# Gathering shifted convolution images with 18 transfers instead of 24, and another order for the first steps, in a float32 network kernel

## The chip, the core and the metric

The kernel runs on one core of a Trainium2 chip. The metric is the device time of one execution in microseconds (us). The engines are named as in the profile: PE is TensorE's matmul stream and PEld its weight loads, DVE is VectorE, ACT is ScalarE, POOL is GpSimd, and SP is SyncE, which here does nothing but issue DMA transfers. A tile's partitions are its rows in on-chip memory; PSUM is the small memory that matmuls write into.

## The reference

Four layers act on an image batch `x` of shape (4, 32, 32, 16). Three of them are the same convolution layer with other weights, and each of these adds to `x` the following function of the normalized `x`:

```python
def conv_ref(inputs, M, W, G):                     # inputs: group-normalized x, NHWC
    first = einsum('ijyx,byxc->bijc', M, inputs)
    # every output place (i, j) has its own 3x3 kernel over 16 channels: 1024 * 16 filters
    shifted = conv(inputs, G)                      # (b, i, j, y, x, c)
    diff = relu(inputs[:, None, None] - shifted)
    second = einsum('ijyx,bijyxc->bijc', W, diff)
    return first - second
```

The layer between the second and the third convolution is an interval layer (scans and two small max-plus steps). It matters here only as other work that runs beside the second convolution.

## The kernel before, in words

The batch of 4 is split in two halves `g` of two images `b` each. There are six phases: convolution layer 0, 1 and 2, each for `g` = 0 and `g` = 1. A phase has 8 chunks `t` of 128 output places, and a chunk has 32 steps, one for each of 16 filters `f` and each of the two images. So a phase is 256 steps, and the whole kernel is 1536 steps. One step multiplies the image, unfolded by the nine taps of the 3x3 kernel, by 128 weight columns. The result `pc` (128 x 1024) is scaled by ACT (L711) and reduced against `W` by DVE in one instruction (L728, `junk`). Four PSUM pairs are there, so step `s` + 4 needs the reduction of step `s` to be done.

To keep float32 accuracy at the fast matmul format, weights and images are split into a high and a low part. Weights come in units of 4 filters, which serve 8 steps. `prep_parts` makes a unit's parts two units ahead: `upper` on DVE (L206), ACT copies, POOL subtractions and copies (L243 to L251), and then two transfers on SP that swap the partition halves (`parts<-parts`, L257), followed by the load of a later unit's raw weights (`raw<-in_g`, L111). The unit after that has the identity tap subtracted by POOL (L220, `prep`) before its own `upper`. The first two units are "plain": their weights are used unsplit, and the first 16 steps take longer matmuls.

The images of the next phase are made beside the steps of the current one. `before_conv` normalizes, writes the padded image to a DRAM tile `xs`, and gathers it back into the tile `raw` of 128 partitions and three slots. Slots 0 and 1 hold eight taps (four groups of 16 channels for each half `h` of the image's width), and slot 2 holds the ninth tap four times over. Then `split`, `place` and `difference` make the high, low and difference images (`ia`, `ib`, `iyz`, and `im9` for the ninth tap).

All of this is one generator, `behind`, that is resumed between steps. `yield n` says how many steps to go before it is resumed. The order written by this generator is the program order on every engine's queue and on SP's. SP has one queue, which runs ahead on its own and stops only where a transfer waits for its data. So the gather's transfers (L419) stand in SP's order between the `parts<-parts` pairs and `raw<-in_g` loads of the weight units. For layers 0 and 1 the gather is written over 12 steps and followed by a pause of 12; for layer 2 it is 12 and 6.

At the start (L936 to L948, `rest_of_start`) the first image comes already unfolded from the host and is normalized in place. `sides` sets the image's edges, `normal` normalizes a slot, `minus_center` subtracts the identity tap from the weights, and `prep_plain_rest` finishes the ninth tap's weights. A few of these stand on DVE and POOL ahead of the first matmuls, and the rest are resumed between the first steps.

Of the kernel before, what the change touches and what calls it, by code (L numbers as in the profile page):

```python
# [16 lines left out]
B, H, C = 4, 32, 16  # L17
NG = 2
GB = B // NG
# [9 lines left out]
RUN = (H - 1) * WP + HW  # L29
LAST = (H - 1) * HW  # L30
TAPS = ((0, 1, 2, 3), (6, 7, 4, 5))
TEMP = 2 * 2 * GB * NH
ROWS = P // H
FU = 4
# [11 lines left out]
def net_kernel(ctx: ExitStack, tc: tile.TileContext, x, xq, xi, convs, iv_w, iv_b, out):  # L46
# [26 lines left out]
    nc = tc.nc  # L73
# [33 lines left out]
    def load_raw(u):  # L107
        if u < n_chunks * NU:
            n = u // NU
            raws[u] = wpool.tile([P, 3, FU, P], F32, tag="raw", bufs=RAWS, name=f"raw_{u}")  # L110
            nc.sync.dma_start(raws[u], convs[phases[n // NT][1]][2][n % NT, u % NU])  # L111
# [16 lines left out]
    raw = const.tile([P, 3, GB, PITCH], F32, name="raw")  # L128
# [48 lines left out]
    def halve(dst, src, mask):  # L177
        nc.scalar.activation(dst, src, AF.Copy, scale=mask[:, 1:2])  # L178

    def halve_rest(dst, src, mask):  # L180
        nc.vector.scalar_tensor_tensor(  # L181
            dst, src, mask[:, 0:1], dst.bitcast(F32), op0=ALU.mult, op1=ALU.add
        )
# [15 lines left out]
    def image(v, x):  # L199
        return v.rearrange("... (y x) -> ... y x", x=x)[..., :HW]  # L200
# [17 lines left out]
    def minus_center(eng, u, s, at, to):  # L218
        f0 = u % NU * FU
        eng.tensor_tensor(  # L220
            raws[u][:, s, at:to], raws[u][:, s, at:to],
            pick[s][:, f0 + at : f0 + to].unsqueeze(2).to_broadcast([P, to - at, P]),
            ALU.subtract,
        )
# [46 lines left out]
    def prep_plain(u, at=0, to=FU, eng=nc.gpsimd):  # L271
        plain_unit(u)
        prep(u, at, to, eng)
        halve(units[u][3][:, at:to], raws[u][:, 2, at:to], low_p)

    def prep_plain_rest(u, at=0, to=FU):
        halve_rest(units[u][3][:, at:to], raws[u][:, 2, at:to], low_p)

    def halves(temp, b):
        v = temp[:, :TEMP].rearrange("p (k s b n) -> p k s b n", k=2, s=2, b=GB)  # L280
        return v[:, 0, :, b], v[:, 1, :, b]

    def split(eng, g, b, temp, name, pause=IDLE):

        ty, tz = halves(temp, b)
        high = upper(image(raw[:, :2, b], WP), 2, f"x{name}{b}")
        yield 1
        for s in range(2):
            eng.tensor_tensor(
                image(tz[:, s], HW), image(raw[:, s, b], WP), image(high[:, s], HW), ALU.subtract  # L290
            )
            yield pause
            nc.scalar.activation(ty[:, s], high[:, s], AF.Copy, scale=EPS)  # L293

    def difference(eng, g, b, s, temp):
        ty, tz = (v.bitcast(F32)[:, s] for v in halves(temp, b))
        eng.tensor_tensor(iyz[g][:, s, b], ty, tz, ALU.subtract)

    def place(g, b, temp):

        parts = halves(temp.bitcast(F32)[:, :TEMP], b)
        da, db = (v[g].bitcast(F32)[:, :, b] for v in (ia, ib))
        for lo, hi in QUARTERS:
            for to, src in zip((lo, hi), parts):
                nc.sync.dma_start(db[to], src[hi])
        for h, (lo, hi) in enumerate(QUARTERS):
            for k, to in enumerate((lo, hi)):
                at = (2 * k * GB + b) * NH + HW * (1 - h)
                pitch = GB * NH + HW * (2 * h - 1)
                src = temp.bitcast(F32)[lo, at : at + 2 * pitch].rearrange("p (s n) -> p s n", s=2)  # L310
                nc.sync.dma_start(da[to, :, :LAST], src[:, :, :LAST])
        yield 1
# [82 lines left out]
    def before_conv(g, layer):  # L395
        xn = work.tile([P, NT, GC], F32, tag="xn", bufs=2, name=f"xn_{g}_{layer}")
        xns[g] = xn
        yield from group_norm(g, f"c{g}{layer}", xn, 1 if layer == 2 else 4)

        nc.vector.transpose(
            xt[g][:, :, 1 : 1 + H], xn
        )
        inner = xs[g][:, :, WP : WP + H * WP].rearrange("p h (t r n) -> p h r t n", r=ROWS, n=WP)
        for r in range(ROWS):
            for h in range(2):
                nc.sync.dma_start(
                    inner[:, h, r], xt[g][GC * r : GC * (r + 1), :, HW * h : HW * h + WP]
                )  # L410
        yield 2
        xsv = xs[g].rearrange("(b c) h n -> c h b n", b=GB)
        for slot, row, tap in [
            (slot, row, tap) for slot in range(2) for row, tap in enumerate(TAPS[slot])
        ] + [(2, row, 8) for row in range(4)]:
            for h in range(2):
                off = tap // 3 * WP + tap % 3
                r0 = 64 * h + C * row
                nc.sync.dma_start(  # L419
                    raw[r0 : r0 + C, slot ^ h if slot < 2 else 2, :, :RUN], xsv[:, h, :, off : off + RUN]  # L420
                )
            yield 1
        yield 6 if layer == 2 else 12
        temp = big.tile([P, 8192], F32R, tag="big", name=f"temp_{g}{layer}")
        for b in range(GB):
            yield from split(nc.gpsimd, g, b, temp, f"{g}{layer}")
            yield IDLE
            halve(image(im9[g][:, b], HW), image(raw[:, 2, b], WP), low_x)
            yield from place(g, b, temp)
            for s in range(2):  # L430
                difference(nc.gpsimd, g, b, s, temp)
            yield 1
            halve_rest(image(im9[g][:, b], HW), image(raw[:, 2, b], WP), low_x)
            yield 4
# [453 lines left out]
    off = const.tile([P, 1], F32, name="off")  # L888
# [21 lines left out]
    def sides(eng, b, slot, only=("left", "right", "top", "bottom")):  # L910

        v = raw[:, slot, b].rearrange("p (y x) -> p y x", x=WP)
        if slot == 2:
            at = v[64:, :, HW - 1]
            eng.tensor_scalar(at, at, mean0[64:, b : b + 1], None, op0=ALU.add)
        for side, at in (
            ("left", v[:, :, 0]), ("right", v[:, :, HW - 1]),
            ("top", v[:, 0, :HW]), ("bottom", v[:, H - 1, :HW]),
        ):
            if side in only and f"{side}{slot}" in keep:  # L920
                k = keep[f"{side}{slot}"]
                eng.tensor_scalar(  # L922
                    at, at, kept[:, k : k + 1], fill[:, b, k : k + 1], op0=ALU.mult, op1=ALU.add
                )

    def normal(eng, b, slot):
        v = raw[:, slot, b, :RUN]
        if eng is nc.scalar:
            eng.activation(v, v, AF.Identity, bias=minus_mean0[:, b : b + 1])
            eng.activation(v, v, AF.Copy, scale=rstd0[:, b : b + 1])  # L930
        else:
            eng.tensor_scalar(  # L932
                v, v, mean0[:, b : b + 1], rstd0[:, b : b + 1], op0=ALU.subtract, op1=ALU.mult
            )

    sides(nc.vector, 0, 0)  # L936
    sides(nc.gpsimd, 0, 2)
    minus_center(nc.gpsimd, 0, 1, 0, F0)
    sides(nc.gpsimd, 0, 1, ("left", "right"))
    nc.vector.reciprocal(rstd0, rstd0)  # L940
    normal(nc.scalar, 0, 2)
    normal(nc.vector, 0, 0)
# [7 lines left out]
    def rest_of_start():  # L950

        nc.sync.dma_start(X[0], x[0])
        load_raw(2)
        load_raw(3)
        prep_plain_rest(0, F0, FU)
        yield 1
        sides(nc.gpsimd, 1, 2)
        sides(nc.gpsimd, 1, 1, ("left", "right"))
        sides(nc.vector, 1, 0)
        sides(nc.vector, 1, 1, ("top", "bottom"))  # L960
        for eng, slot in ((nc.scalar, 2), (nc.vector, 0), (nc.vector, 1)):
            normal(eng, 1, slot)
        halve(image(im9[0][:, 1], HW), image(raw[:, 2, 1], WP), low_x)
        halve_rest(image(im9[0][:, 1], HW), image(raw[:, 2, 1], WP), low_x)
        prep_plain(1)
        prep(2)
        yield 1
        prep_plain_rest(1)
        yield 1
        temp = first.bitcast(F32R)[:, used:]  # L970
        for b in range(GB):
            yield from split(nc.vector, 0, b, temp, "00", 1)
            yield from place(0, b, temp)
            for s in range(2):
                difference(nc.vector, 0, b, s, temp)
            yield 1
        nc.gpsimd.memset(zero, 0.0)
        nc.vector.memset(part, 0.0)
        zeros(0)
        xns[0] = work.tile([P, NT, GC], F32, tag="xn", bufs=2, name="xn_00")  # L980
        yield from group_norm(0, "c00", xns[0], 4, CALM)
# [83 lines left out]
```

## Time and profile before

| | us |
|---|---|
| median of 3 runs (2466.83 to 2468.67) | 2467.36 |
| the profiled execution's own time | 2469.47 |
| its span, first to last instruction | 2467.4 |
| PE busy | 2457.5 (100%) |
| PE weight loads busy | 2056.1 (83%) |
| DVE busy | 2075.6 (84%) |
| ACT busy | 1873.6 (76%) |
| POOL busy | 1594.7 (65%) |
| DMA queue q1 (SP), share of 16 engines | 53.4% |
| granted PE clock | 1.000 |

Busy times are sums over an engine's instructions. PE's matmuls are pipelined and their ends are modelled, so a PE that is 100% busy can still lose time to waits; the steps' start times tell more. The DMA share is the time that packets took on 16 DMA engines. A "packet" of the profile is one run of bytes that one DMA engine moves.

### The profile page before, as it was taken

What the parts mean: (1) busy time and instruction counts of PE and PEld (TensorE: products, weight loads), DVE (VectorE), ACT (ScalarE), POOL (GpSimd) and SP (SyncE); (2) the same over time, 40 slices, a digit from 0 to 9 for tenths busy, and PEclk for the clock granted to TensorE, in tenths of its full rate; (3) what the DMA queues carried; (4) which work ended last, traced back from release to release, by engine and by line L of the source; (5) the groups of instructions that cost most, each with busy time, mean ns of one, the idle gap of its engine ahead of it and who ended that gap; (6) DMA issues with size and microseconds to landing.
All of it is one profiled execution on the core that took longest, in us unless ns stands there. A gap on an engine that the chain in (4) does not pass through costs nothing.

```text
span 2467.4 us, 58148 instructions
## 1 busy us (share of the span) xinstructions
PE 2457.5 (100%) x21928; PEld 2056.1 (83%) x21928; DVE 2075.6 (84%) x3631; ACT 1873.6 (76%) x2164; POOL 1594.7 (65%) x1864
## 2 busy tenths in 40 slices
PE   9999999999999999999999999999999999999999
PEld 5888888888888888888888888888889888888887
DVE  9888878888888888878898888888888888788887
ACT  4777777787777778767777777777777787677776
POOL 5767665676666667555576876776777675555552
PEclk9999999999999999999999999999999999999999
DMA  7456654485444467644554454664444476554452
GB/s 202 138 156 162 185 179 137 127 200 141 133 143 135 137 168 186 199 113 137 138 139 131 126 142 136 168 179 137 128 136 136 128 206 179 147 148 137 138 137 55
DMA packets 96906, 366.92 MB, mean 149 GB/s; under 512 B 25712, under 2 KB 30704, under 8 KB 96624
## 3 DMA queue, kind: packets, MB, share of 16 engines
q1 hardware_dynamic: 96064, 362.79, 53.4%
q8 instruction: 172, 2.82, 0.5%
q14 instruction: 110, 0.90, 0.1%
q10 hardware_dynamic: 432, 0.39, 0.1%
q0 software_dynamic: 128, 0.02, 0.0%
HBM read 199.78 MB, written 1.02 MB: 81 GB/s over the span
## 4 chain that ended last, share of the span: by engine, by line
PE 96%; DVE 1%; DMA 1%; ACT 1%; issue 1%; POOL 0%; ACTq 0%; DVEq 0%; POOLq 0%
PE pc L675 95%; PE pf L451 1%; DVE junk L728 1%; DMA raw<-in_g 0%; ACT pc L711 0%; DMA first<-in_g 0%; ACT temp L293 0%; PE ps_l L585 0%; DMA ib<-first 0%; PE ps_r L600 0%; DVE raw L922 0%; DVE im L181 0%; DVE W L181 0%; DVE raw L932 0%; ACT im L178 0%
## 5 line engine op out<-in xcount | busy, mean ns | idle before, releaser
L728 DVE SCALAR_TENSOR_TENSOR junk<-pc,WT 128x1024 f32<-128x1024 f32 x1536 | 1879.3, 1224 | 354.4 <-PE pc L675 295.2
L711 ACT ACTIVATE pc<-pc 128x1024 f32<-128x1024 f32 x1520 | 1532.2, 1008 | 560.5 <-PE pc L675 525.2
L675 PE MATMUL pc<-iyz,parts 64*128 64x512 f32 x6080 | 943.3, 387 | 2.1 <-ACT pc L711 1.6
L675 PE MATMUL pc<-ib,parts 64*128 64x512 f32 x6080 | 945.2, 387 | 0.2
L675 PE MATMUL pc<-ia,parts 64*128 64x496 f32 x6080 | 920.8, 379 | 0.0
L675 PEld LDWEIGHTS pc<-ia,parts 64*128 64x128 f32 x6080 | 578.8, 184 | 111.7
L675 PEld LDWEIGHTS pc<-ib,parts 64*128 64x128 f32 x6080 | 576.9, 184 | 108.4 <-issue 5.0
L675 PEld LDWEIGHTS pc<-iyz,parts 64*128 64x128 f32 x6080 | 577.3, 184 | 97.9 <-ACT pc L711 7.3
L675 PE MATMUL pc<-im,W 64*128 64x496 f32 x3072 | 598.6, 383 | 0.0
L243 POOL TENSOR_TENSOR parts<-raw,upper_w 128x512 fp32r<-128x512 f32 x190 | 249.5, 1313 | 522.7 <-DVE upper_w L206 440.9
L675 PEld LDWEIGHTS pc<-im,W 64*128 64x128 f32 x3072 | 292.7, 184 | 59.9 <-issue 3.3
L249 POOL CAST parts<-parts 32x512 fp32r<-32x512 f32 x380 | 231.7, 610 | 36.0 <-ACT parts L246 17.4
L247 POOL TENSOR_TENSOR parts<-parts 128x512 fp32r<-128x512 f32 x190 | 247.5, 1303 | 1.6 <-ACT parts L242 1.5
L244 POOL TENSOR_TENSOR W<-W,raw 128x512 fp32r<-128x512 f32 x190 | 247.8, 1304 | 0.3 <-ACT W L178 0.3
L251 POOL CAST parts<-upper_w 32x512 fp32r<-32x512 f32 x380 | 233.1, 613 | 22.8
L220 POOL TENSOR_TENSOR raw<-raw,ident 128x512 f32<-128x512 f32 x190 | 197.9, 1042 | 59.3 <-DMA raw<-in_g 35.4
L178 ACT ACTIVATE W<-raw,low_w 128x512 fp32r<-128x512 f32 x190 | 136.2, 717 | 3.7 <-DMA raw<-in_g 3.7
L728 DVE DVE_READ_ACCUMULATOR junk<-pc,WT 128x1 f32 x1536 | 127.6, 83 | 0.0
L242 ACT ACTIVATE parts<-upper_w 128x512 fp32r<-128x512 f32 x190 | 118.7, 624 | 3.8 <-DVE upper_w L206 3.7
L246 ACT CAST parts<-upper_w 128x512 fp32r<-128x512 f32 x190 | 116.1, 611 | 0.0
L743 POOL TENSOR_SCALAR acc<-acc 128x32 f32<-128x32 f32 x40 | 15.7, 392 | 133.9 <-DVE junk L728 132.1
L206 DVE TENSOR_SCALAR upper_w<-raw 128x512 int32<-128x512 int32 x190 | 82.1, 432 | 10.2 <-POOL raw L220 9.9
(158 smaller groups left out, 481.2 us busy)
## 6 DMA issues: line engine op xcount, KB each, us to landing
raw<-in_g SPq DMA_DIRECT2D x190, 768.0 KB, 7.2
parts<-parts SPq DMA_DIRECT2D x380, 384.0 KB, 5.0
WT<-in_w SPq DMA_DIRECT2D x48, 512.0 KB, 4.8
MT<-in_mt SPq DMA_DIRECT2D x24, 512.0 KB, 7.5
raw<-xs SPq DMA_DIRECT2D x120, 71.8 KB, 3.5
ib<-temp SPq DMA_DIRECT2D x40, 128.0 KB, 7.4
ia<-temp SPq DMA_DIRECT2D x40, 124.0 KB, 6.0
ib<-first SPq DMA_DIRECT2D x8, 128.0 KB, 4.0
```

Source lines behind the costliest of these rows:

```text
L178: nc.scalar.activation(dst, src, AF.Copy, scale=mask[:, 1:2])
L220: eng.tensor_tensor(raws[u][:, s, at:to], raws[u][:, s, at:to], pick[s][:, f0 + at : f0 + to].unsqueeze(2).to_broadcast([P, to - at, P]), ...
L242: nc.scalar.activation(WD, high, AF.Copy, scale=-EPS)
L243: nc.gpsimd.tensor_tensor(WL, w8, high, ALU.subtract)
L244: nc.gpsimd.tensor_tensor(W9, W9.bitcast(F32), src[:, 2], ALU.add)
L246: nc.scalar.copy(WU, high)
L247: nc.gpsimd.tensor_tensor(WD, WD.bitcast(F32), WL.bitcast(F32), ALU.add)
L249: nc.gpsimd.tensor_copy(WU[hi], WL[lo].bitcast(F32))
L251: nc.gpsimd.tensor_copy(WL[lo], high[hi])
L675: nc.tensor.matmul(ps[:, h, at : at + n], lhsT=w[r], rhs=v[r] if n == NH else v[r][:, :n], start=first and k == 0, stop=k == len(pairs) - ...
L711: nc.scalar.activation(ps, ps, AF.Copy, scale=1.0 + EPS)
L728: nc.vector.scalar_tensor_tensor(junk, ps.rearrange("p h n -> p (h n)"), 0.0, chunks[n], op0=ALU.min, op1=ALU.mult, accum_out=accs[phase][ ...
```

## The change

The gather in `before_conv` is rewritten. Before, each transfer moved one tap: 16 channels of both images into 16 partitions. Now adjacent groups of partitions whose taps lie at a constant distance are moved by one transfer for one image: three taps (48 partitions), one tap for both images as before (16 partitions), twice two taps (32 partitions), and the ninth tap's four copies (64 partitions). To do this, a leading dimension of 3, 2, 2 or 4 is put in front of the source's access pattern, with a distance of one element between taps, or of zero for the copies. That makes 18 transfers for each gather in place of 24 in the code before. For layers 0 and 1 they are written two for every second step, over 18 steps and with a pause of 6; for layer 2 two for each step, over 9 steps and with a pause of 9. The sum of the pauses is the same as before.

At the start, POOL sets the left and right edges of slot 1 before it subtracts the identity tap, not after. `prep_plain_rest(1)` comes one step later, and the differences of the first phase's two images come together after both images have been placed.

```diff
+RUNS = ((0, 0, 3, 0, 1), (0, 3, 1, 3, 1), (1, 0, 2, 6, 1), (1, 2, 2, 4, 1), (2, 0, 4, 8, 0))
...
-        for slot, row, tap in [
-            (slot, row, tap) for slot in range(2) for row, tap in enumerate(TAPS[slot])
-        ] + [(2, row, 8) for row in range(4)]:
+        for b, (slot, row, n, tap, by) in [
+            (b, run) for b in range(GB) for run in RUNS if run[2] > 1 or b == 0
+        ]:
             for h in range(2):
+                at = raw[64 * h + C * row :, slot ^ h if slot < 2 else 2, :, :RUN]
                 off = tap // 3 * WP + tap % 3
-                r0 = 64 * h + C * row
-                nc.sync.dma_start(
-                    raw[r0 : r0 + C, slot ^ h if slot < 2 else 2, :, :RUN], xsv[:, h, :, off : off + RUN]
-                )
-            yield 1
-        yield 6 if layer == 2 else 12
+                src = xsv[:, h, :, off : off + RUN]
+                if n > 1:
+                    src = src[:, b]
+                    src = bass.AP(src.tensor, src.offset, [[by, n]] + [list(d) for d in src.ap])
+                    dst = at[: n * C, b]
+                else:
+                    dst = at[:C]
+                nc.sync.dma_start(dst, src)
+            yield 1 if layer == 2 else 2
+        yield 9 if layer == 2 else 6
...
     sides(nc.gpsimd, 0, 2)
+    sides(nc.gpsimd, 0, 1, ("left", "right"))
     minus_center(nc.gpsimd, 0, 1, 0, F0)
-    sides(nc.gpsimd, 0, 1, ("left", "right"))
...
         prep(2)
-        yield 1
+        yield 2
         prep_plain_rest(1)
-        yield 1
...
             yield from place(0, b, temp)
+        for b in range(GB):
             for s in range(2):
                 difference(nc.vector, 0, b, s, temp)
             yield 1
```

## The prediction

> **What bounds the kernel now.** I read the page first: PE is busy for the whole span, and the chain that ended last is PE's for 96% of it.
>
> ```profile
> PE 2457.5 (100%) x21928; PEld 2056.1 (83%) x21928; DVE 2075.6 (84%) x3631; ACT 1873.6 (76%) x2164; POOL 1594.7 (65%) x1864
> PE 96%; DVE 1%; DMA 1%; ACT 1%; issue 1%; POOL 0%; ACTq 0%; DVEq 0%; POOLq 0%
> raw<-xs SPq DMA_DIRECT2D x120, 71.8 KB, 3.5
> ```
>
> The change removes no matmul, so it can only remove or add waits of PE. PE's timeline gives their size. An undisturbed step takes 1.57 us (a weight unit of eight: 12.54). From the starts of the 1536 steps I added what lies above that, leaving out the plain steps' longer matmuls, the `pf` matmuls and the interval layer: 3.4 us of waits in the first 52 us and some 5 us elsewhere, of which 1.4 at 920.7 and 0.2 to 0.4 each at a dozen places. So a gain is capped near 8 us (0.3%). A loss has no such cap.
>
> The last line is the gather: 120 transfers in five gathers, so 24 each (not 36). Its order on SP is seen in the DMA queue's timeline, here ahead of phase 4 (columns: start, us of issuing, line, transfer, count):
>
> ```profile
> 1562.49 1.11 SPq L257 DMA_DIRECT2D parts<-parts  x2
> 1563.64 1.91 SPq L111 DMA_DIRECT2D raw<-in_g  x1
> 1565.66 9.34 SPq L419 DMA_DIRECT2D raw<-xs  x14
> 1575.17 1.10 SPq L257 DMA_DIRECT2D parts<-parts  x2
> 1576.38 1.15 SPq L111 DMA_DIRECT2D raw<-in_g  x1
> 1577.57 9.35 SPq L419 DMA_DIRECT2D raw<-xs  x10
> 1587.08 1.11 SPq L257 DMA_DIRECT2D parts<-parts  x2
> ```
>
> The weight units' transfers stand behind gather transfers. PE's timeline shows how little room they have: the unit whose halves are swapped at 1575.17 starts here, 7.8 us later.
>
> ```profile
> 1582.96 0.62 PE L675 MATMUL pc<-ib,parts 64*128 64x512 f32 x4
> ```
>
> In a quiet stretch this distance is 14 to 15 us. Ahead of phase 3 (SP timeline, then the chain of waits) the same order already costs PE time:
>
> ```profile
> 896.28 11.86 SPq L419 DMA_DIRECT2D raw<-xs  x16
> 909.51 1.25 SPq L111 DMA_DIRECT2D raw<-in_g  x1
> ...
> 909.51 11.36 DMA raw<-in_g
> 921.01 1.05 POOL raw L220
> ```
>
> Sixteen gather transfers hold SP until 908.14; the load behind them lands at 920.87, POOL and DVE (`upper`, due at 919.27) wait, and PE loses the 1.4 us.
>
> Last, how transfers are spread, from the DMA view of 620 to 700 us (nothing is gathered there) and of 1565.6 to 1587:
>
> ```profile
> DMA packets 2138, 10.67 MB, mean 133 GB/s; under 512 B 327, under 2 KB 327, under 8 KB 2128
> parts<-parts SPq DMA_DIRECT2D x12, 384.0 KB, 4.4
> raw<-in_g SPq DMA_DIRECT2D x6, 768.0 KB, 7.0
> WT<-in_w SPq DMA_DIRECT2D x2, 512.0 KB, 4.5
> ...
> DMA packets 1585, 4.36 MB, mean 204 GB/s; under 512 B 437, under 2 KB 437, under 8 KB 1582
> q1 hardware_dynamic: 1582, 4.33, 75.3%
> ```
>
> 20 transfers leave 327 small packets, 16 each; the second window's 27 leave 437, again 16. So every transfer ends on 16 engines, and the outermost dimension of each, on both sides, is a multiple of 16 (partitions or channels).
>
> **The gather.** The bytes stay: 768 rows of 2296 B per gather. But the new sources begin with a dimension of 3, 2, 2 or 4. The trace has no such transfer, so I bound it: its rows are shared by all 16 engines (48 rows on each per gather, as now), or go through one engine (up to 768). Between these far ends I take equal slabs of the outermost dimension, because multiples of 16 in that place are what goes with 16 engines in every row: 16 rows on each of the first 3, 2, 2 or 4 engines. With (0,3,1) unchanged at 2 rows, the first two engines then carry 4 transfers x 4 runs x 16 + 4 = 260 rows per gather in place of 48. I take an engine's queue as served in order (the load of 909.51, behind sixteen gather transfers, took 11.36 us to land, against the page's median of 7.2), so the swaps and loads behind the gather wait for their share on these two.
>
> [...]
>
> A row's time on one engine: in 1565.6 to 1587 a packet takes 0.753 x 16 x 21.4 / 1585 = 0.163 us for 2.75 KB on average, or 0.136 for 2296 B; the window's best slices (394 GB/s, 24.6 per engine) give 0.093. Few engines draw at once, so I take 0.10, near the low end.
>
> Layer 2 (two gathers): the pauses put the first 7 of 9 entries, 14 transfers, where 14 stood, but with 6 x 2 x 16 + 4 = 196 rows on the first engine: 19.6 us (18.2 to 26.7). Its service starts at about 1567.5, behind the `raw<-in_g` of 1563.64, and ends at 1587.1; the swap's own rows (8 of 6 KB, about 2.4 us) and about 1.2 us to the signal make it 1590.7, where PE needs it at 1583.2. PE waits 7.5 us (6 to 15). The load behind it is as late, in the shadow of the same wait. The second batch (64 rows) fits in the next unit. Two gathers: **+15** (12 to 30). `split` reads the first image at 1590, 8 us after its rows.
>
> Layers 0 and 1 (three gathers): spread over 18 steps, 4, 8 and 6 transfers stand between the units' groups: 36, 128 and 96 rows, so 3.6, 12.8 and 9.6 us against a unit of 12.54 that also holds 4.4 us of the units' own rows. In phase 0, counting from 206.2, the swaps land near 231.0 and 245.0; PE starts those units at 230.82 and 243.35 (the second matmul pair needs them 0.2 later): 1.4 late. The other two gathers have about 1 us more room: some 1.4 together. **+2.8** (0 to 22). The 1.4 us at 920 go, because 8 transfers stand there instead of 16: **-1.4**. The images' own deadline (step 24) holds: last rows at about 241, second image split at 256.
>
> SP issues 30 transfers fewer at about 0.5 us; that is covered, as SP waits for data afterwards anyway.
>
> **The first steps.** Timeline: POOL waits until 7.62 for a load, subtracts until 8.53, then sets edges until 9.31; DVE's last edges and normalization follow, and PE's second matmul group idles 1.25 us until 10.55.
>
> ```profile
> 8.53 0.78 POOL L922 TENSOR_SCALAR raw<-raw,kept,fill 128x32 f32<-128x32 f32 x2
> 10.55 1.13 PE L675 MATMUL pc<-raw,first 64*128 64x512 f32 x4 [1.25 <-issue]
> 13.21 0.42 POOL L915 TENSOR_SCALAR raw<-raw,mean 64x32 f32<-64x32 f32 x1 [3.90 <-DMA raw<-in_xi]
> ```
>
> With the edges first (7.07 to 7.85) DVE normalizes by 9.2 and PE goes on at 9.3; the ninth tap's matmuls move from 11.56 to 10.45: 1.1 us. It is given back: the second image lands at 13.2 whatever is done before, DVE's chain from there (edges, normalization, ninth tap until 18.27, then the reduction of step 1 until 19.42) hardly moves, and step 5 waits for that reduction's PSUM pair, at 19.5 as against 19.66. Then the ninth weights (1.53 us on DVE) leave the place before step 2's reduction, but `upper` behind them waits for POOL's subtraction until 20.32: DVE idles 0.9. Step 6 starts 0.45 earlier; step 7, now behind the ninth weights, about 0.75 later. The differences (2.13 and 1.35 us on DVE) move four steps back and none; DVE has little slack until 51 us, so this only shifts who is late. Together **+0.5**, between -1.2 (all of the first gain stays) and +1.2.
>
> **Sum.** +15 + 2.8 - 1.4 + 0.5 = +16.9 us. The profiled execution took 2469.47, 2.1 more than its span and than the median; the waits add to each alike, so on the median 2467.4 + 16.9 = 2484.3.
>
> [...]
>
> **The rivals.** (1) The new transfers keep 16 engines. For: the same bytes and row size. Then 18 issues only relieve SP: -1.4 - 0.4 (small DVE waits in the two layer-2 gathers) + 0.5: 2466.1, no measurable change (about 0.2%, 4.9 us, is what a measurement of this kernel can tell from none). (2) Not slower but faster: as (1), and the gather's late data were also behind the dozen small waits. It needs most of the 8 us; the places at 260, 544 and 947 show ACT queued behind `split`'s copies, which stay in their steps: 2461. It decides if no row of a gather delays a unit. (3) One engine carries a whole new transfer: 516 rows instead of 196 in layer 2's batch, 32 us more twice, and about 38 in each of three: near 2660. Against it: only the outermost size sets it apart from all rows shown. (4) Fewer transfers than said: it is 24 to 18, not 36 to 18; this is already in the sum.
>
> **The numbers.** Forecast 0.77, (1) 0.17, (2) 0.04, (3) 0.02. The forecast's own range runs from 2477 (0.093 us per row, first gain kept: +12 + 0 - 1.4 - 1.2) to 2519 (0.136: +30 + 22 - 1.4 + 1.2). To hold 8 in 10 it reaches down to case (1): 2466 to 2520. Slower by over 0.2%: 0.77; within it, case (1) and the weakest end of the forecast against little else: 0.19; faster 0.04.
>
> **What would show it.** Right: `raw<-xs` x90 with a median landing far above 3.5 us; far fewer small packets than 16 for each of them; `parts<-parts` landings above 15 us in the gathers; PE idle before `ib` matmuls near 1583 and 1990 by 6 to 9 us each, and 1 to 2 us near 231 to 245; no wait at 921; first `im` matmul near 10.45 and step 7 later than 24.45. Wrong: 16 small packets for each gather transfer and landings below 5 us; then the time stays.

## The result, and the profile after

The changed kernel takes 2533.95 us (median of 5 runs, 2531.91 to 2536.75) against 2467.36 before: 1.027 times as long, 95% interval 1.0258 to 1.0282. The forecast was 2484.3, with a range up to 2520. The direction and the mechanism held, but the loss is 66.6 us and not 16.9.

The page of the changed kernel, from its busy times, DMA packets, chain and groups (in this kernel the lines stand up to six lower than before, so PE's L675 is L681):

```profile
PE 2480.4 (98%) x21928; PEld 2066.3 (82%) x21928; DVE 2083.8 (82%) x3631; ACT 1874.4 (74%) x2164; POOL 1596.8 (63%) x1864
DMA packets 95365, 366.91 MB, mean 145 GB/s; under 512 B 24172, under 2 KB 29164, under 8 KB 95084
PE 86%; DMA 8%; SPq 2%; DVE 1%; issue 1%; POOL 1%; ACT 0%; DVEq 0%; POOLq 0%; ACTq 0%
L681 PE MATMUL pc<-ib,parts 64*128 64x512 f32 x6080 | 964.8, 389 | 42.5 <-DMA parts<-parts 36.7
```

PE is no longer busy throughout, the chain that ended last holds 10% of DMA and SP (1% of DMA before), and PE stands idle ahead of the first matmuls that need swapped weights (`parts<-parts`). PE's waits over the whole span (total, times, longest) say the same; before, no wait of PE for `parts<-parts` was listed:

```profile
PE pc L681 <- DMA parts<-parts: 36.7, 12, 10.2
PE pc L681 <- DVE junk L734: 6.3, 10, 1.1
```

The gather ahead of phase 4, on SP's timeline; it answers to the lines from 1562.49 of before:

```profile
1599.66 2.39 SPq L258 DMA_DIRECT2D parts<-parts  x2
1602.09 0.59 SPq L112 DMA_DIRECT2D raw<-in_g  x1
1602.79 12.26 SPq L427 DMA_DIRECT2D raw<-xs  x14
1615.43 1.92 SPq L258 DMA_DIRECT2D parts<-parts  x2
1619.62 0.35 SPq L112 DMA_DIRECT2D raw<-in_g  x1
```

Then PE's timeline, the chain of waits there, and the DMA view of 1600 to 1640 (one character or number for each us):

```profile
1629.95 0.79 PE L681 MATMUL pc<-ib,parts 64*128 64x512 f32 x1 [9.37 <-DMA parts<-parts]
1631.53 0.79 PE L681 MATMUL pc<-ib,parts 64*128 64x512 f32 x1 [0.79 <-DMA parts<-parts]
```

```profile
1608.05 8.77 DMA raw<-xs
...
1616.84 14.65 DMA parts<-parts
```

```profile
DMA  5989988611123231599995961122299999962111
GB/s 110 198 203 197 227 362 296 175 73 78 67 80 96 83 104 78 162 213 271 200 134 216 319 190 52 51 67 87 81 210 226 221 201 332 239 184 95 59 53 56
```

The swap issued at 1615.43 lets PE go on only 14.5 us later. For long stretches ahead of it the DMA engines are 10 to 30% busy, the work of two to five of the sixteen, and move 50 to 100 GB/s. Where the number falls to about 50 it fits two engines at the 24.6 GB/s that each has in the best slices of before (394 GB/s over 16).

The page no longer gives a landing time for the gather's transfers, but the trace's semaphore updates do (the trace keeps the time of each update that a DMA makes). From issue to last update a gather transfer takes 12.6 us in the median, 3.5 before. Before, each has 16 updates. Of the 90 now, 10 have 16; each of the others has one about 1 to 2 us after its issue and then only 2 (40 transfers), 3 (20) or 4 (20) more. The swap issued at 1615.43 has all 16: thirteen within 4.1 us, one after 5.9, and the last two after 14.3 and 14.5. Read as one update for each engine that a transfer ran on, this says that two of the sixteen DMA engines hold up the whole swap.

What happens after such a wait is seen in PE's granted clock (the number after POOL's count), here around the same place:

```profile
1620.00:1630.00 10.00, 0.63 (x7) 0.21 (x3) 1.35 (x4) 0.73 (x1) 0.00 (x0) 0.71 0.52 141
1630.00:1633.00 3.00, 2.21 (x9) 1.45 (x11) 0.00 (x0) 0.00 (x0) 0.00 (x0) 0.50 0.97 216
1633.00:1636.00 3.00, 3.00 (x24) 2.46 (x22) 1.23 (x2) 1.61 (x2) 0.84 (x1) 0.77 0.93 252
1636.00:1640.00 4.00, 4.00 (x39) 3.15 (x35) 3.64 (x7) 3.61 (x6) 2.78 (x4) 1.00 0.17 66
```

PE restarts at clock 0.50 and has 1.00 again from 1634.36 on. At the other gathers a whole step of 2.84 to 2.95 us follows the wait where 1.57 is usual.

From the starts of all 1536 steps, the two profiles differ as follows (sum 64.2 of the spans' 64.6 us; PE's waits are those listed for the gather's window):

| stretch | later by, us | of it PE waits for swaps | for DVE |
|---|---|---|---|
| first 20 steps | 5.4 | - | - |
| gather ahead of phase 1 | 10.6 | 5.3 | 1.4 |
| phase 2 | 11.15 | 5.0 | 1.3 |
| phase 3 | 10.1 | 5.4 | 1.2 |
| phase 4 (layer 2) | 12.55 | 10.2 | - |
| phase 5 (layer 2) | 14.45 | 10.8 | - |

### The profile page after: what moved, and what is told of

The parts are those of the page before. It is cut to its first block, busy times and chain, and to the rows that moved or that the text cites. A ratio compares the mean times of both kernels' runs of the same rounds, so it can differ in the third digit from the quotient of the medians.

```text
span 2532.0 us, 58118 instructions
## 1 busy us (share of the span) xinstructions
PE 2480.4 (98%) x21928; PEld 2066.3 (82%) x21928; DVE 2083.8 (82%) x3631; ACT 1874.4 (74%) x2164; POOL 1596.8 (63%) x1864
## 4 chain that ended last, share of the span: by engine, by line
PE 86%; DMA 8%; SPq 2%; DVE 1%; issue 1%; POOL 1%; ACT 0%; DVEq 0%; POOLq 0%; ACTq 0%
PE pc L681 85%; DMA raw<-xs 4%; DMA raw<-in_g 2%; DMA parts<-parts 2%; DVE junk L734 1%; PE pf L457 1%; SPq L427 1%; SPq L409 1%; DMA first<-in_g 0%; DMA xs<-xt 0%; POOL raw L221 0%; ACT pc L717 0%; SPq L258 0%; POOL parts L250 0%; POOL parts L248 0%
## 5 line engine op out<-in xcount | busy, mean ns | idle before, releaser
L681 PE MATMUL pc<-ib,parts 64*128 64x512 f32 x6080 | 964.8, 389 | 42.5 <-DMA parts<-parts 36.7
L681 PE MATMUL pc<-iyz,parts 64*128 64x512 f32 x6080 | 957.2, 388 | 0.9 <-ACT pc L717 0.4
L681 PE MATMUL pc<-ia,parts 64*128 64x496 f32 x6080 | 937.0, 381 | 0.0
L681 PEld LDWEIGHTS pc<-ib,parts 64*128 64x128 f32 x6080 | 587.8, 185 | 160.4 <-DMA parts<-parts 42.0
L681 PEld LDWEIGHTS pc<-ia,parts 64*128 64x128 f32 x6080 | 589.3, 185 | 112.5
L681 PEld LDWEIGHTS pc<-iyz,parts 64*128 64x128 f32 x6080 | 586.0, 185 | 98.8 <-ACT pc L717 5.6
L681 PE MATMUL pc<-im,W 64*128 64x496 f32 x3072 | 609.9, 385 | 0.0
L681 PEld LDWEIGHTS pc<-im,W 64*128 64x128 f32 x3072 | 302.3, 185 | 60.3 <-issue 3.5
```

The lines of the kernel that those rows point to most:

```text
L681: nc.tensor.matmul(ps[:, h, at : at + n], lhsT=w[r], rhs=v[r] if n == NH else v[r][:, :n], start=first and k == 0, stop=k == len(pairs) - ...
```

## The experiments

The theory: a merged transfer runs on as many engines as its source's outermost size (2, 3 or 4, the number of its later updates), so its rows take long on those, and the weight units' swaps and loads, which stand behind it in SP's queue, come late. Rivals: it is the order or the pauses, the number of transfers, or the first steps. "Gather" below means the change's gather with its pauses in the kernel before. Ratios are against the kernel before.

**The two halves of the change.** First the gather alone, then the three first-step edits alone, each as in the diff of the change.

> The kernel before with the gather and its pauses alone changed. Theory (few DMA engines carry the new transfers): nearly all of the loss is here. In the profile of the changed kernel the five gathers cost 10.3, 10.9, 9.7, 12.1 and 13.9 us more than before, together some 57 to 59, so 2524 to 2527. Rival (the first steps hold a good part of the loss, because they shift the whole schedule): clearly less, below 2515.

2531.86 us, ratio 1.0255 (1.024 to 1.027), somewhat above the expected range. From its waits of PE:

```profile
PE pc L681 <- DMA parts<-parts: 38.7, 15, 9.8
```

> The kernel before with the three edits of the first steps alone. Theory: the 5.4 us by which step 20 starts later in the changed kernel's profile stay, so 2471 to 2474. Rival (PE's slower first matmuls in that profile were a chance of that one execution): within 1.5 us of before, 2466 to 2469.

2473.59 us, ratio 1.0021 (1.0012 to 1.003); 5.0 us are lost by step 20. The halves add up to the whole. The 1.4 us wait at 921 of before is missing here too, where nothing of the gather is changed, and in each of the four first-step runs below; so its going isn't the gather's doing.

**Same transfers, other order of the source's dimensions.** The runs' 48, 32 or 64 partitions stay; only the 16 channels become the source's outermost dimension. (Taps and channels then land in each other's partitions, so this kernel times the transfers and doesn't compute the reference.)

```diff
-src = bass.AP(src.tensor, src.offset, [[by, n]] + [list(d) for d in src.ap])
+src = bass.AP(src.tensor, src.offset, [list(src.ap[0]), [by, n], list(src.ap[1])])
```

> As gather_only, with the first two dimensions of each new source exchanged: 16 channels first, then 2, 3 or 4 taps. Number of transfers, bytes, rows, partitions, order and pauses stay. Taps and channels land in each other's partitions, so the convolutions of phases 1 to 5 multiply the wrong pairs. [...] Rival (large transfers for one image, the new order, or the pauses are what costs): still above 2510.

2468.68 us, ratio 1.000 (0.999 to 1.0009): the gather's loss is gone; 2464 to 2468 was expected by the theory. No wait of PE for swaps is left, there are 1060 more small packets than in the changed kernel, and the gather's transfers have a landing time in the page again (KB, us):

```profile
DMA packets 96425, 366.91 MB, mean 149 GB/s; under 512 B 25232, under 2 KB 30224, under 8 KB 96144
raw<-xs SPq DMA_DIRECT2D x50, 71.8 KB, 5.6
raw<-xs SPq DMA_DIRECT2D x20, 143.5 KB, 5.1
```

That is the count which the theory gives: 40 pairs, 20 triples and 20 runs of four that leave 2, 3 and 4 small packets each, and 16 each with the channels outermost, differ by 40 x 14 + 20 x 13 + 20 x 12 = 1060. All 90 transfers have 16 semaphore updates again. So in these runs the source's outermost size decides (2, 3 and 4 against 16 updates); the order, the pauses and these 18 larger transfers cost nothing by themselves.

**Transfers of one tap and one image.** 46 for each gather, each with 16 channels outermost.

```diff
-dst = at[: n * C, b]
+for k in range(n):
+    one = bass.AP(src.tensor, src.offset + k * by, [list(d) for d in src.ap])
+    nc.sync.dma_start(at[k * C : k * C + C, b], one)
...
-nc.sync.dma_start(dst, src)
```

> As gather_only, each run of n taps issued as n transfers of 16 partitions for one image, in the same places of the order: 46 transfers per gather instead of 18. Theory: every transfer has 16 channels outermost and runs on 16 engines; SP spends about 14 us more on issuing per gather than with 18, so 2466 to 2475. Rival (order, pauses or one image at a time): above 2510.

Missed: 2506.61 us, ratio 1.0159 (1.0142 to 1.0176). The landing is short, but SP takes 0.6 us for each, and the swap waits for its turn (SP's timeline, then the page):

```profile
212.76 13.51 SPq L425 DMA_DIRECT2D raw<-xs  x22
226.43 1.30 SPq L258 DMA_DIRECT2D parts<-parts  x2
```

```profile
raw<-xs SPq DMA_DIRECT2D x220, 35.9 KB, 1.9
```

So the swaps behind a gather can be late for either reason: too few engines, or too many transfers ahead.

**Part of the merging.** The ninth tap's four copies alone, then the pairs of slot 1 alone. `one(slot)` stands for the slot's four single runs, which go as before; pauses are set so that their sum stays (in layers 0 and 1 the first is written over 20 steps, the second over 12).

```diff
-RUNS = ((0, 0, 3, 0, 1), (0, 3, 1, 3, 1), (1, 0, 2, 6, 1), (1, 2, 2, 4, 1), (2, 0, 4, 8, 0))
+RUNS = (*one(0), *one(1), (2, 0, 4, 8, 0))
```

> Of the gather only the ninth tap's four copies are merged (four channels of 16 partitions each in one transfer for one image); eight taps go as before. 20 transfers, two for each step or second step, first steps as before. Theory (a new transfer runs on as many engines as its outermost size, and what counts is the rows that stand on the first engines): per gather 64 + 16x2 = 96 rows on the first four engines instead of 48, against 260 in the changed kernel. In layer 2 the merged transfers come after the first 14, in the second unit's time, 64 rows or about 9 us at 0.14 us, most of which fits there: +1 to +5 us per gather, +5 to +20 in all, time 2472 to 2488. Rival (any merged transfer costs the same, by itself and not by its rows; 4 of 16 merged ones per gather): a quarter of the 61 us, 2482 to 2485. Rival (the loss is the pauses' order and the number of issues, not the engines): 2467 to 2469.

2476.92 us, ratio 1.0038 (1.0024 to 1.0051).

```profile
PE pc L681 <- DMA parts<-parts: 1.7, 2, 1.1
```

```diff
+RUNS = (*one(0), (1, 0, 2, 6, 1), (1, 2, 2, 4, 1), *one(2))
```

> Only the two pairs of slot 1 are merged (two taps of 16 channels in one transfer for one image, eight such transfers), the rest as before: 24 transfers, first steps as before. Theory: 128 + 16x2 = 160 rows on the first two engines per gather, against 48 before and 260 in the changed kernel; in layer 2 these stand in the first batch of 14, 10 us more on two engines than on 16: +5 to +9 us per gather, +20 to +40 in all, time 2487 to 2507, more than with the ninth tap alone. Rival (each merged transfer costs alike; 8 of 16 merged): half of 61, 2496 to 2500. Rival (not the engines): 2467 to 2469.

2504.9 us, ratio 1.015 (1.0135 to 1.0165).

```profile
PE pc L681 <- DMA parts<-parts: 21.6, 10, 4.2
```

With 48, 96, 160 and 260 rows for each gather on the engines that hold most of them, by the theory's count, PE waits 0, 1.7, 21.6 and 38.7 us for swaps. Some 96 rows still fit beside the units here, and 160 don't. The rhythm and the place in the gather differ between these runs too: in layer 2 the four copies come last, behind the first 14 transfers, and how much that saves was not separated.

**Half of each row**, of the change's gather.

```diff
-at = raw[64 * h + C * row :, slot ^ h if slot < 2 else 2, :, :RUN]
+at = raw[64 * h + C * row :, slot ^ h if slot < 2 else 2, :, : RUN // 2]
...
-src = xsv[:, h, :, off : off + RUN]
+src = xsv[:, h, :, off : off + RUN // 2]
```

> The changed kernel's gather and pauses in the kernel before, with each row of the gather cut to its first half (1148 B instead of 2296; the second half of each shifted image is not gathered, so later phases use old values there). Number of rows, transfers, engines and order stay. If what delays the swaps is the time to move the rows' bytes on two to four engines (24.6 GB/s for each, 0.093 us per row, and half of that now): PE's first wait per gather of 3 to 10 us loses 5 to 10 us, so next to nothing stays; 2467 to 2482. If it is a cost per row, whatever its length: near the 2531.9 of gather_only, at least 2515.

2476.23 us, ratio 1.003 (1.0018 to 1.0042). What delays the swaps is mostly bytes on few engines and not a cost per row; a half row takes 0.051 us on its engine in the median of the trace's DMA records, a whole one 0.093:

```profile
PE pc L681 <- DMA parts<-parts: 4.3, 3, 2.0
```

**The same gather on ACT's queue.** First the issuer alone; then with a longer pause between the store of the image and the gather, too, and other pauses in and behind it.

```diff
-nc.sync.dma_start(dst, src)
+nc.scalar.dma_start(dst, src)
```

```diff
-yield 2
+yield 5 if layer == 2 else 6
...
-    yield 1 if layer == 2 else 2
-yield 9 if layer == 2 else 6
+    yield 1 if layer == 2 and b else 2
+yield 3 if layer == 2 else 2
```

> The changed kernel's gather and pauses in the kernel before, but issued by ACT on its own queue, so that the weight units' swaps and loads on SP's queue don't stand behind it. If the order within SP's queue is what costs: swaps land within 6 us even during a gather, and PE's waits for them fall from 8 to 12 us per gather to under 2; what is left is ACT's own time for issuing 18 transfers, some 0.5 us each, or 9 us per gather on an engine that is 76% busy, of which up to 5 may show in PE: time 2470 to 2490. If it is the engines themselves that are held (their rows are served first whatever queue they come from): swaps still land 10 us late, and the time is 2520 to 2545.

2539.2 us, ratio 1.029 (1.0273 to 1.0307): the rival's time. PE no longer waits for swaps at all, but for ACT (47.9 us), which stands first for the store of the image and then at its own transfers. The swaps still land late: in the gathers up to 11.6 us after their issue by the trace's semaphore updates, where 5.1 is usual and the changed kernel has up to 14.6.

> As gather_act, but the gather begins three to four steps later after the store of the image, so that ACT no longer stands waiting for it, and in layer 2 the first five entries are two steps apart; the pause behind is shorter by as much (layer 2: the whole gather two steps longer). [...] If the merged gather costs the same wherever it is queued, because its rows occupy the first engines: 10 to 12 us per gather again, 2520 to 2540.

2529.46 us, ratio 1.0247 (1.023 to 1.0264): again the time expected if the merged gather costs the same wherever it is queued. With the order in SP's queue as the cause, 2475 to 2505 was expected. Its SP timeline, PE's and ACT's in layer 2's gather, and the waits of ACT and PE over the span:

```profile
1610.61 1.24 SPq L258 DMA_DIRECT2D parts<-parts  x2
```

```profile
1617.78 1.22 PE L681 MATMUL pc<-iyz,parts 64*128 64x512 f32 x4 [3.91 <-ACT pc L717]
...
1634.90 0.62 PE L681 MATMUL pc<-ib,parts 64*128 64x512 f32 x4
```

```profile
1612.97 3.65 ACTq L427 DMA_DIRECT2D raw<-xs  x2
1616.72 1.01 ACT L717 ACTIVATE pc<-pc 128x1024 f32<-128x1024 f32 x1 [4.76 <-DMA raw<-xs]
```

```profile
ACT pc L717 <- DMA raw<-xs: 42.5, 12, 4.9
PE pc L681 <- ACT pc L717: 38.6, 23, 3.9
```

No wait of PE for a swap is listed, but the swaps aren't quick. The two of 1610.61 and 1611.12 have 13 of their 16 updates within 5.5 us and the last after 8.4 and 9.6; in this run's gathers it comes after up to 11.9. PE doesn't notice, as the unit that needs these two starts only at 1634.90: ACT holds up the steps ahead of it. So in another queue the swaps are less late than the 14.5 us of the changed kernel, and still late; how much of the lateness is their place in one queue, and how much the engines that both queues share, these two runs don't separate.

What holds ACT is seen in the semaphores that the transfers update. Those of SP and ACT use eight in turn, and each issue held here starts just after the last update of the transfer that had its semaphore before: the one issued at 1612.97 after that of 1603.14, whose last update comes at 1612.95, and the next, at 1615.99, after that of 1606.03, last update 1615.97. So a gather that lands late holds its issuer, here ACT for 3 to 5 us and PE behind it. SP is held in the same way in the changed kernel: the swap of 1616.84 follows the landing, at 1616.82, of the gather transfer of 1608.05, which the chain of waits above shows, and two such waits of 0.7 and 0.8 us stand within SP's 12.26 us for 14 transfers (10.29 with the channels outermost). A gather on ACT's queue with the channels outermost was not run, so what the issuing alone costs ACT is open.

**The first steps, edit by edit.** The edges before the subtraction; the ninth weights a step later; the differences together; and these with one step more between the first image's `place` and the second's `split`:

```diff
-    minus_center(nc.gpsimd, 0, 1, 0, F0)
     sides(nc.gpsimd, 0, 1, ("left", "right"))
+    minus_center(nc.gpsimd, 0, 1, 0, F0)
...
-        yield 1
+        yield 2
         prep_plain_rest(1)
-        yield 1
...
             yield from place(0, b, temp)
+            yield 1                          # only with the gap
+        for b in range(GB):
             for s in range(2):
```

> Of the three first-step edits only the first: POOL sets slot 1's left and right edges before it subtracts the identity tap. Theory (the lost time comes from the differences that no longer stand between the two images): this edit moves step 20 by -0.5 to +0.5 us, and the time stays, 2466 to 2470. Rival (the early edits delay DVE's chain from the second image on, through the first weights' subtraction coming late): step 20 later by 2 to 5 us, time 2470 to 2473.

> Only the ninth tap's weights of the second unit come one step later. Theory (the differences): step 7 about 0.5 to 0.9 us later, step 20 by 0 to +1 us, time 2467 to 2470. Rival (the ninth weights, now behind a reduction and ahead of the second image's work, push all that follows): step 20 later by 2 to 5 us, time 2470 to 2473.

> Only the differences of the first phase's two images come together, after both placements. Theory: DVE's split of the second image waits about 2.2 us for the first image's placement (ia<-first), which the first image's differences covered, and the four differences, back to back beside POOL's work, take 2.5 to 2.9 us each instead of 2.1 and 1.35; step 20 later by 3.5 to 5 us, time 2470.5 to 2473.5. Rival (the two other edits): step 20 within 1 us of the kernel before, time 2467 to 2469.

> As the one before (differences together), with one step more between the first image's placement and the second image's split, so that another step's reduction covers the wait for the placement. If the wait of 2.2 us is what costs, step 20 is later by 0 to 2 us only, and the time 2467 to 2470. If it is the slower differences, step 20 is later by 3 to 5 us as without the gap, time 2470.5 to 2473.5.

| | us, ratio | step 20 later by |
|---|---|---|
| edges | 2469.59, 1.0001 (0.9991 to 1.0011) | -0.3 |
| ninth weights | 2469.87, 1.0002 (0.9993 to 1.0012) | +1.5 |
| differences | 2473.48, 1.0019 (1.001 to 1.0028) | +3.6 |
| differences, with a gap | 2469.12, 1.0001 (0.9992 to 1.001) | -0.2 |

The differences are the cost. The other rows are too small to read: PE's matmuls on a blank tile ahead of the first step take 1.87 to 3.55 us from one execution to the next, and the first `im` matmul comes between 10.99 and 12.80 us in these four. DVE's timeline, first of the run with the differences together, then of the one with the gap:

```profile
31.80 0.69 DVE L289 TENSOR_TENSOR first<-raw,upper_x 128x512 fp32r<-128x512 f32 x1 [2.05 <-DMA ia<-first]
...
36.78 2.53 DVE L297 TENSOR_TENSOR iyz<-first 128x512 fp32r<-128x512 f32 x2
...
40.38 2.91 DVE L297 TENSOR_TENSOR iyz<-first 128x512 fp32r<-128x512 f32 x2
```

```profile
32.79 0.69 DVE L289 TENSOR_TENSOR first<-raw,upper_x 128x512 fp32r<-128x512 f32 x1 [0.83 <-DMA ia<-first]
...
39.30 1.70 DVE L297 TENSOR_TENSOR iyz<-first 128x512 fp32r<-128x512 f32 x2
...
42.07 1.70 DVE L297 TENSOR_TENSOR iyz<-first 128x512 fp32r<-128x512 f32 x2
```

The second image's `split` waits for the first image's placement, which the first image's differences used to cover. One step more covers it again, and the differences are also shorter at the later time.

**A spread without merging.** The 24 transfers of before, in layers 0 and 1 over 18 steps with a pause of 6, and the edges first.

```diff
-            yield 1
-        yield 6 if layer == 2 else 12
+            yield 1 if layer == 2 else 1 + row % 2
+        yield 6
```

> The 24 transfers of the kernel before, in layers 0 and 1 spread over 18 steps instead of 12 (with a pause of 6 instead of 12), and the first edit of the first steps (edges before the subtraction). Theory: the wait of 1.4 us at 921 goes and nothing else changes: 2464.5 to 2467.5, not to be told from the kernel before. Rival (the spread itself is what costs in the changed kernel): above 2475.

2467.58 us, ratio 0.9998 (0.9989 to 1.0008): no difference from before. Of all kernels run here none beats it measurably.

## Why the prediction was right in kind and wrong in size

**Engines by the outermost size: right.** Slabs on 3, 2, 2 and 4 engines, which the prediction took between its two far bounds, are what the runs show: 2, 3 and 4 updates per transfer, no cost for the same transfers with 16 outermost (2468.68 us), and waits that grow with the rows per engine (0, 1.7, 21.6 and 38.7 us). That all slabs begin on the same first engines was an assumption of the sum. It fits the swap's last two updates, 14.3 and 14.5 us after its issue; which engines these are no run here shows, as the trace doesn't number them. Of the signs that the prediction named, the 90 late gather transfers, the missing small packets and PE's waits before `ib` matmuls came; the swaps took up to 14.6 us and not over 15. Rivals (1), (2) and (3) fall; (4) stood in the sum.

**Row time: mis-sized.** The prediction took 0.10 us, near its low end, because few engines would draw at once. From the first gather transfer's issue at 1602.79 to PE's restart on the second half at 1631.53 are 28.74 us. Less the prediction's own estimates of 1.8 to the start of service, 2.4 for the swap and 1.2 for the signal, 23.3 us remain for 196 rows: 0.119 each. No run shows these 1.8 and 1.2: the trace of the changed kernel has the first of these rows start 3.9 us after that issue, and that of before has the last update of an undisturbed swap (issued at 2422.55) 0.8 us after the end of its last packet. The 2.4 fits 8 packets of 6 KB at their median of 0.30. The gather ahead of phase 1 gives the same to the restart at 241.10: 29.28 us from 211.82, less 1.8, 1.2, two swaps (4.8) and a load's share of an engine (768 KB / 16 / 24.6 GB/s = 2.0), are 19.5 us for 164 rows, 0.119, an estimate like the first. The DMA records of 1604 to 1640 show both ends: with up to four of them under way a row takes 0.097 us on average, with thirteen or more 0.139, when the units' traffic runs beside it; the mean of all is 0.115. So 0.136, the mean that the prediction took from a busy window, was as near as its 0.10. With 0.119, layer 2 waits 7.5 + 196 x 0.019 = 11.2 (measured 10.2 and 10.8). Ahead of phase 1 the unit that was forecast just in time (231.0 for 230.82) is late by 164 x 0.019 = 3.1 (measured 2.91 + 1.11), and the next, forecast 1.4 late, waits another 0.57 + 0.71.

**Layers 0 and 1: the step that failed most.** +2.8 us was forecast for three gathers and 31.9 came. It rested on a margin of about 1 us each at a row time from the low end, so that 20% more time per row turned "just in time" into 5 us of waiting three times (15.7 in all). The bound that the prediction itself gave (22) was nearer.

**What follows a wait: left out of the sum.** Of the five gathers' 58.9 us, 36.7 are waits for swaps and 3.9 waits for DVE, whose `upper` comes late behind a late load; the 1.4 us of before at 921 that are not there belong to them as well. So 58.9 + 1.4 - 36.7 - 3.9 = 19.7 us are steps that run longer without waiting, 2.4 to 4.9 for each gather. The sum has no term for them. Before, the clock is 1.00 from 4.55 us to 2465.56, the end of the steps. Now it falls in all five gathers (windows at the times of the trace's clock changes, the clock after POOL's count):

```profile
241.72:245.14 3.42, 3.42 (x20) 2.76 (x18) 1.57 (x3) 1.01 (x1) 1.04 (x1) 0.50 0.48 144
535.27:542.10 6.83, 5.96 (x29) 4.62 (x30) 1.57 (x3) 2.15 (x3) 2.10 (x2) 0.50 0.67 157
948.28:955.11 6.83, 5.91 (x25) 4.47 (x27) 1.57 (x3) 1.52 (x2) 1.47 (x2) 0.50 0.61 147
1624.12:1634.36 10.24, 3.62 (x15) 2.59 (x17) 0.00 (x0) 1.01 (x1) 0.00 (x0) 0.50 0.62 156
2043.96:2057.62 13.66, 6.24 (x27) 4.68 (x29) 1.57 (x3) 1.85 (x2) 1.80 (x2) 0.50 0.61 163
```

PE is busy for 25.15 us at half the clock, where a matmul of 64x512 took 0.79 us (0.389 on average). That costs half of the time, 12.6 us, as an estimate; the other 7.1 us are open. By the same estimate it is 1.7 to 3.1 us for each of the five gathers, and in the first the clock fell after waits of 2.91 and 1.11 us.

**The first steps: +0.5 forecast, +5.4 measured.** The step that failed is "this only shifts who is late". At their old place the first image's differences (2.13 us) stood where DVE would otherwise have waited for that image's placement, and so cost next to nothing. That cover was not looked for. DVE's timeline of the changed kernel has it, and PE waits ahead of its first split unit:

```profile
33.74 0.69 DVE L290 TENSOR_TENSOR first<-raw,upper_x 128x512 fp32r<-128x512 f32 x1 [2.12 <-DMA ia<-first]
```

```profile
46.46 0.82 PE L681 MATMUL pc<-ib,parts 64*128 64x512 f32 x4 [1.81 <-POOL parts L252]
```

The edges' gain did not come: the first `im` matmul is at 11.55 and not at 10.45, as PE's own matmuls on a blank tile took 3.11 us in this execution, 1.87 in that of before (3.49 with the edges alone); whether the gain is there in an execution with quick ones, no run shows. Step 7 is later, as said, by 0.76 us.

**The wait at 921.** Its -1.4 was counted as the change's; in the runs above it is gone with the old gather, too. That the forecast's -1.4 came is luck.

Put together: 17.8 us of forecast waits, 18.9 more mainly by the row time, 19.7 after the waits, 3.9 by DVE and 5.4 at the start, less the 1.4 at 921, are the 64.2 measured between the profiles (a split of what was measured, and no second forecast).

## What to carry to other kernels

Merging transfers by putting a small dimension in front of a large one took them from sixteen updates to two, three or four here, and their landing from 3.5 to 12.6 us: look at the source's outermost size before counting issues, and try the large one outermost (2468.68 against 2531.86 us here). The swap behind such transfers in the same queue landed after up to 14.6 us; from another queue it was less late, up to 11.9, and the issuer of the gather was held. A queue with a margin of 1 us per unit should be costed at the pessimistic row time, and a gather's waits of PE at their length plus the 2.4 to 4.9 us by which the steps were slower here. Before work is moved off an engine, ask which wait it was covering.

## What was not expected of the hardware

After the waits of the five gathers the granted clock was 0.50 for 3.41, 6.83, 6.83, 10.24 and 13.65 us in the changed kernel's profile. A wait of only 1.81 us (ahead of 46.46) was followed by 3.41 us of it as well. A gather's waits cost 2.4 to 4.9 us beyond their own length.

The description of the kernel has SP stop only where a transfer waits for its data; it also stops elsewhere. In the traces of before and of the changed kernel the transfers of SP and ACT use eight semaphores in turn, and none is issued before the last update of the transfer that had its semaphore before; in the changed kernel the closest of these 897 issues starts 0.016 us after it. Before, with gather transfers that land in 3.5 us in the median, no wait of SP for them is listed; in the changed kernel, with 12.6 us, it waits 34.7 us for them at the gather (L427) and 13.2 at the weights' loads (L112). On ACT's queue the issue of two transfers then took up to 4.96 us, where 1.15 is usual.
